# Key/query projection in two 64-column halves, routing behind the first value, an earlier DCT tile and one load queue, in a transformer layer on one core

## The chip, the core and the metric

The kernel runs on one core of one Trainium2 chip. Times are device microseconds (us) of a whole execution. A kernel is timed by several executions; I quote medians with the range. Shares, waits and starts come from one profiled execution of each kernel. Every execution compared here was fast: none was over 1.5% above the fastest of its kernel.

In the profile PE is the matmul engine (PEld is its weight load, which runs beside it: in the kernel before, PE is busy for 98% of the span and PEld for 57%), DVE the vector engine, ACT the scalar engine, POOL GpSimd, and SP the engine that issues most of the transfers. "L181" is line 181 of that kernel's source. Lines shift between kernels, so the text says what each line is.

## The reference

64 audio clips of 80,000 samples become 157 frames of 512 samples each. Cut to what matters:

```python
h = einsum('bfh,kh->bfk', frames, dct_512)          # DCT of each frame
x = layernorm(h)
key   = exp(1j * pi * tanh(x @ Wk + bk))            # 4 sets x 8 planes = 32 columns
query = exp(1j * pi * tanh(x @ Wq + bq))            # 32 columns
V = x @ Wv + bv
for s in range(4):                                  # causal sums of key * V, read by conj(query)
    total += softmax(set_weights)[s] * Re(sum_planes(cumsum(key_s * V) * conj(query_s)))
gate  = sigmoid(x @ Wg + bg)
total = gate * total + (1 - gate) * pos_contrib     # same sums with fixed position phases
h = h + x + (total / norm) @ Wo + bo
x2 = layernorm(h)
scores = softmax(mean_over_frames(x2) @ Wg_ffn + bg_ffn)
e = argmax(scores)                                  # one expert of 16 for each clip
h = h + scores[e] * (x2 @ We[e] + be[e])
```

## The kernel before

All is in 4-byte floats. The 64 clips run in 16 groups of four. A group has five tiles of 128 tokens: the first 128 frames of each clip, and the 29 last ones of all four clips together (the "tails"). DVE and POOL first fold each frame (additions and subtractions of its parts), and PE then does the DCT of the folded frame. Groups are woven together: while the attention of group g runs, the DCT and the first norm of g+1 are made ahead of it, and the experts of g-1 behind it. The causal sums are computed as masked score matrices of phases: scores, times V.

The projection makes 128 columns: key and query, each twice, so that one activation turns one copy into cosines and the other into sines.

```python
def project(g):
    s = S[g]
    s["u"] = u = p1.tile([P, GB, LP], F32, tag="tT", name="u")[:, :, :L]
    ps = psum()
    turns = turn_x2(g - 1)            # transposes of the second norm's tiles
    for k in range(2):                # k: two clips at a time, 314 columns
        next(turns, None)
        next(turns, None)
        for c in range(C):
            nc.tensor.matmul(ps[:, k, : 2 * L], wkq[:, c, :],
                             s["xT"][:, c, 2 * k : 2 * k + 2, :L], ...)
    for _ in turns:
        pass
    nc.scalar.activation(u..., by_halves(ps), AF.Tanh, bias=bkq)

def phasors(g):
    u = S[g].pop("u")
    nc.vector.scalar_tensor_tensor(u, u, sgn, u, ALU.mult, ALU.max)
    rows = slice(2 * F, P)
    nc.scalar.activation(qf[: 2 * F, :, :L], u[rows], AF.Sin, bias=off[rows], scale=scl[rows])
    rows = slice(0, 2 * F)
    nc.scalar.activation(kf[rows, :, :L], u[rows], AF.Sin, bias=off[rows], scale=scl[rows])
    nc.scalar.activation(by_tail(kf_t[rows]), u[rows, :, P:], AF.Sin, ...)
```

Here PE's results go to the memory PSUM, and ACT and DVE empty it (in the profile before, ACT takes 0.79 us for a gate part's 128x628 and DVE 0.32 us for a score's 128x157). Two pools of it matter: `psum()` gives one of three large buffers (two banks each), `bank()` one of two small ones. Transposes, scores and the routing use the small ones.

```python
def scores(i):
    ps = bank()
    nc.tensor.matmul(ps[:, :L], kf[:, i, :P], qf[:, i, :L], start=True, stop=True)
    nc.vector.tensor_tensor(att[i][:, 0, :], ps[:, :L], hmask, ALU.mult)
    ...
# the group's loop, cut to what the change touches
    project(g)
    if behind:
        route(g - 1)                  # 16 matmuls, four 32-column parts of the array at once: 32 records in 1.27 us
    phasors(g)
    if behind:
        route_sum(g - 1)              # DVE
        ...                           # folds of the next frames
        weigh()                       # DVE scales the queries
        for m in range(NM):
            value(g, m)
            if m == 0:
                route_spread(g - 1)
            ...
    for m in range(NM):
        if ahead:
            embed(g + 1, m)           # DCT tile
            if m > 0:
                turn(g + 1, m - 1)    # its transposes; ACT copies the bank away
            embed_ln(g + 1, m)        # statistics, norm, and the addition of bo on POOL
            load_frame(g + 2, m)
        if m < GB:
            gate_part(g, m)
        if m < 2:
            scores(2 * m)
            scores(2 * m + 1)
        ...
```

## Time and profile before

| | before |
|---|---|
| median of 4 executions | 1605.51 us (1604.59 to 1606.74) |
| profiled span, granted PE clock | 1603.6 us, 0.997 |
| distance of two groups (mean from group 2 to 15) | 97.98 us |
| start of the first projection | 46.59 us |
| first projection of group 0 to that of group 1, then to group 2 | 61.19, 99.70 us |

The last rows are read from the starts of the projection's first matmul in each group. As PE is almost never idle, these distances are what the kernel costs, and they can be compared between kernels to some 0.02 us. 14 equal groups make a small term visible that the whole time, with its spread of 2 us, hides. One stretch of the chain of waits is shown here (start, duration, what), where the reads of the attention (L437) meet those of the tails (L450):

```profile
259.21 1.07 PE mm L437 x4
...
260.90 0.50 DVE tT L426
...
261.54 1.02 PE mm L450 x4
262.56 0.44 PE tr L160 x4
```

PE had to wait here until DVE had emptied a large buffer: 3.35 us pass from 259.21 to 262.56. (The chain counts four of the eight L437; the other four run while DVE works, and PE then stands idle for 0.21 us by the timeline.)

### The profile page before, as it was taken

To read this page: it belongs to the slowest core of one execution; us is meant where nothing else is said; L and a number is where in the kernel's file an instruction comes from. 1 tells how busy PE (TensorE), PEld (TensorE's weight loads), DVE (VectorE), ACT (ScalarE), POOL (GpSimd) and SP (SyncE) were. 2 spreads that over 40 slices of the span, in tenths; PEclk is the share of its full clock that TensorE was granted. 3 is DMA by queue.
4 is the path that set the end of the run, shared out by engine and by line. 5 is a ranking of instruction groups with operands and counts; after the bars stand their busy time and mean duration, and the time that the engine had idled before them with its cause. 6 is when DMAs were issued, how large, how long until landed. Compare 5 with 4: busy or idle time off the path is not lost.

```text
span 1603.6 us, 17469 instructions
## 1 busy us (share of the span) xinstructions
PE 1565.5 (98%) x6224; PEld 920.9 (57%) x6224; DVE 713.1 (44%) x1738; ACT 425.2 (27%) x598; POOL 528.8 (33%) x947
## 2 busy tenths in 40 slices
PE   7999999999999999999999999999999999999997
PEld 4656556464564746647465574655646466474652
DVE  4354544435444444444345444354443544444253
ACT  3433123231322313223132232212323132231210
POOL 4424324243332333323234242332424333233032
PEclk9999999999999999999999999999999999999999
DMA  5103131131312313132231411313114131212216
GB/s 181 29 5 132 46 138 46 46 138 55 129 40 77 107 62 129 33 122 62 65 126 40 150 39 54 131 53 131 46 46 138 57 127 40 79 72 62 109 33 203
DMA packets 42998, 135.39 MB, mean 84 GB/s; under 512 B 8016, under 2 KB 8416, under 8 KB 34336
## 3 DMA queue, kind: packets, MB, share of 16 engines
q0 software_dynamic: 15616, 88.09, 16.1%
q1 hardware_dynamic: 26088, 45.66, 9.2%
q8 instruction: 50, 0.82, 0.2%
q10 hardware_dynamic: 1208, 0.52, 0.2%
q14 instruction: 36, 0.29, 0.0%
HBM read 113.67 MB, written 20.58 MB: 84 GB/s over the span
## 4 chain that ended last, share of the span: by engine, by line
PE 89%; DMA 1%; DVE 1%; ACT 1%; issue 1%; POOL 0%; DVEq 0%; POOLq 0%
PE mm L179 45%; PE mm L400 16%; PE mm L437 7%; PE tr L160 4%; PE mm L369 4%; PE mm L196 4%; PE mm L584 3%; PE mm L194 2%; PE mm L450 2%; PE tr L489 1%; PE tr L412 1%; DMA out<-be 1%; ACT x2T L168 1%; DMA be<-in_be,expi 1%; DVE tT L426 0%
## 5 line engine op out<-in xcount | busy, mean ns | idle before, releaser
L400 PE MATMUL mm<-xT,wg 128*128 128x314 f32 x1024 | 281.2, 426 | 0.0
L179 PE MATMUL mm<-wv,xT 128*128 128x512 f32 x512 | 228.4, 598 | 0.9 <-ACT xT L166 0.9
L400 PEld LDWEIGHTS mm<-xT,wg 128*128 128x128 f32 x1024 | 189.1, 188 | 69.7 <-issue 0.5
L179 PE MATMUL mm<-we,x2T 128*128 128x512 f32 x512 | 223.0, 593 | 0.1
L179 PE MATMUL mm<-wo,tT 128*128 128x512 f32 x512 | 222.3, 592 | 0.0
L179 PEld LDWEIGHTS mm<-we,x2T 128*128 128x128 f32 x512 | 97.0, 190 | 122.5 <-issue 118.6
L469 ACT ACTIVATE x<-res,shift,rstd 128x512 f32<-128x512 f32 x80 | 65.1, 813 | 383.7 <-POOL shift L154 383.7
L179 PEld LDWEIGHTS mm<-wo,tT 128*128 128x128 f32 x512 | 97.3, 190 | 117.2 <-issue 114.8
L179 PEld LDWEIGHTS mm<-wv,xT 128*128 128x128 f32 x512 | 95.1, 191 | 112.5 <-issue 110.4
L93 POOL TENSOR_TENSOR frame<-frame 128x256 f32<-128x256 f32 x80 | 58.5, 739 | 292.6 <-DVE even L92 281.7
L151 POOL TENSOR_SCALAR rstd<-mv 128x1 f32<-128x1 f32 x160 | 42.1, 263 | 330.8 <-DVE mv L149 327.9
L437 PE MATMUL mm<-att,v 128*128 128x314 f32 x512 | 143.2, 427 | 0.0
L209 POOL TENSOR_TENSOR res<-res,bo 128x512 f32<-128x512 f32 x80 | 101.7, 1272 | 113.3 <-ACT res L208 110.0
L206 ACT ACTIVATE x<-mm,shift,rstd 128x512 f32<-128x512 f32 x80 | 62.2, 777 | 270.9 <-POOL shift L154 270.7
L466 DVE TENSOR_TENSOR res<-mm,res 128x512 f32<-128x512 f32 x80 | 55.3, 692 | 150.6 <-PE mm L179 150.6
L437 PEld LDWEIGHTS mm<-att,v 128*128 128x128 f32 x512 | 94.9, 190 | 31.2
L592 DVE SCALAR_TENSOR_TENSOR be<-mm,gate,be 128x512 f32<-128x512 f32 x80 | 59.9, 750 | 116.9 <-PE mm L179 76.4
L562 POOL DMA_INDIRECT be<-in_be,expi x80 | 83.3, 1041 | 63.8 <-DMA out<-be 33.0
L147 DVE BATCH_NORM_STATS2 st<-mm 128x6 f32<-128x512 f32 x80 | 55.9, 699 | 106.7 <-PE mm L196 106.7
L152 POOL TENSOR_TENSOR rstd<-rstd,power 128x1 f32<-128x1 f32 x160 | 96.3, 602 | 13.3
L160 PE MATMUL tr<-ident,x 128*128 128x128 f32 x640 | 92.0, 274 | 5.7 <-ACT x L206 3.1
L160 PEld LDWEIGHTS tr<-ident,x 128*128 128x128 f32 x640 | 76.1, 141 | 35.0 <-issue 14.7
(117 smaller groups left out, 1794.3 us busy)
## 6 DMA issues: line engine op xcount, KB each, us to landing
frame<-in_frames SPq DMA_DIRECT2D x80, 256.0 KB
out<-be SPq DMA_DIRECT2D x64, 256.0 KB
out<-be SPq DMA_DIRECT2D x60, 32.0 KB
out<-be SPq DMA_DIRECT2D x60, 26.0 KB
be<-in_be,expi POOLq DMA_INDIRECT x80, 4.1
wv<-in_wv SPq DMA_DIRECT2D x1, 1024.0 KB
wg<-in_wg SPq DMA_DIRECT2D x1, 1024.0 KB
wo<-in_wo SPq DMA_DIRECT2D x1, 1024.0 KB
```

The source lines that it names most:

```text
L152: nc.gpsimd.tensor_tensor(rstd, rstd, power, ALU.pow)
L160: nc.tensor.transpose(tr[:, c * P : (c + 1) * P], x[:, c * P : (c + 1) * P], ident)
L179: nc.tensor.matmul(ps, lhs(c), w[:, c, :], start=(c == 0), stop=(c == C - 1))
L196: nc.tensor.matmul(by_r[:, 1::2, :], ft[:, i, :], dct_o[:, i, :], start=(i == 0), stop=(i == 1))
L206: nc.scalar.activation(x, h, AF.Identity, bias=shift, scale=rstd)
L209: nc.gpsimd.tensor_tensor(r, r, bo, ALU.add)
L369: nc.tensor.matmul(ps[:, k, : 2 * L], wkq[:, c, :], s["xT"][:, c, 2 * k : 2 * k + 2, :L], start=(c == 0), stop=(c == C - 1),)
L400: nc.tensor.matmul(ps[:, k, : 2 * L], wg[:, c, o * P : (o + 1) * P], s["xT"][:, c, 2 * k : 2 * k + 2, :L], start=(c == 0), stop=(c == C - 1),)
L437: nc.tensor.matmul(ps[:, c, : 2 * L], s["v", i][:, cols], att[i], start=True, stop=True)
L469: nc.scalar.activation(x, r, AF.Identity, bias=shift, scale=rstd)
L562: nc.gpsimd.indirect_dma_start(out=be, out_offset=None, in_=a["be"], in_offset=bass.IndirectOffsetOnAxis(ap=s["expi"][:, m : m + 1], axis=0),)
L592: nc.vector.scalar_tensor_tensor(o, ps, s["gate"][:, m : m + 1], o, ALU.mult, ALU.add)
```

## The change

It has four intents. The projection computes only 64 columns, key and query once, and the two pairs of clips are meant to use the two column halves of the array at the same time. The cosines and sines then come from eight smaller activations in place of three. The routing moves behind the first value matmul, which needs nothing new, so that PE doesn't wait for the last copy of x2. The DCT of tile m+1 goes ahead of gate part m, and the transposes of tile m behind it. Last, all loads use one queue, the additions of `bo` in group 0 move off POOL's early work, and there are more warm-up matmuls. Along with this the folds and the scaling of the queries (`weigh`) have other places among the values.

```diff
     def project(g):
-        ps = psum()
+        ps = psum()[:, 0, :]
         turns = turn_x2(g - 1)
-        for k in range(2):
-            next(turns, None)
-            next(turns, None)
-            for c in range(C):
+        for c in range(C):
+            if c % 2 == 0:
+                next(turns, None)
+                next(turns, None)
+            for k in range(2):
                 nc.tensor.matmul(
-                    ps[:, k, : 2 * L],
+                    ps[2 * F * k : 2 * F * (k + 1), : 2 * L],
 ...
     def phasors(g):
-        nc.vector.scalar_tensor_tensor(u, u, sgn, u, ALU.mult, ALU.max)
-        ... (three sines)
+        nc.vector.scalar_tensor_tensor(u[:, 1], u[:, 0], -1.0, u[:, 0], ALU.mult, ALU.max)
+        for n, to in ((0, kf), (1, qf)):
+            for k in range(2):
+                ... (a sine of u[rows, 0] and one of u[rows, 1], 32 rows each)
+        nc.gpsimd.tensor_copy(by_tail(kf_t[: 2 * F]), kf[: 2 * F, :, P:L])
 ...
         project(g)
-        if behind:
-            route(g - 1)
         phasors(g)
-            route_sum(g - 1)
             for m in range(NM):
                 value(g, m)
                 if m == 0:
+                    route(g - 1)
+                    fold_twice(g + 1, 1)
+                    keep_value(g, m)
+                    route_sum(g - 1)
+                elif m == 1:
                     route_spread(g - 1)
 ...
         for m in range(NM):
+            for n in (0, 1) if m == 0 else (m + 1,):
+                if ahead and n < NM:
+                    embed(g + 1, n)
+                    embed_ln(g + 1, n)
+                    load_frame(g + 2, n)
             if ahead:
-                embed(g + 1, m)
-                if m > 0:
-                    turn(g + 1, m - 1)
-                embed_ln(g + 1, m)
-                load_frame(g + 2, m)
+                add_bo(g + 1, m)
             if m < GB:
                 gate_part(g, m)
+                if ahead:
+                    turn(g + 1, m)
             if m < 2:
                 scores(2 * m)
                 scores(2 * m + 1)
 ... (load queue, warm-up, add_bo and the order of the start-up cut)
```

More of the change, by code (lines that the diff above doesn't have):

```diff
@@ L64, in audio_tower, with load @@
     ps_tr = pool("ps_tr", 2, space=bass.MemoryType.PSUM)
-    def load(name, shape, src=None, queue=nc.sync):
+    def load(name, shape, src=None):
         t = const.tile(shape, F32, name=name, tag=name)
-        queue.dma_start(out=t, in_=a[name] if src is None else src)
+        nc.sync.dma_start(out=t, in_=a[name] if src is None else src)
         return t
@@ L111, in audio_tower @@
     load_frame(0, 4)
-    bv = load("bv", [P, D], a["bv"].partition_broadcast(P), queue=nc.scalar)
-    freqs = load("freqs", [2 * PLANES, 1], queue=nc.scalar)
-    ptrig = load("ptrig", [2 * PLANES, 3], queue=nc.scalar)
-    pos = load("pos", [2 * PLANES, LP], queue=nc.scalar)
-    posw = load("posw", [P, 1], a["posw"].partition_broadcast(P), queue=nc.scalar)
-    setw = load("setw", [2 * F, SETS], a["setw"].partition_broadcast(2 * F), queue=nc.scalar)
-    setsel = load("setsel", [2 * F, SETS], queue=nc.scalar)
-    trig = load("trig", [P, 3], queue=nc.scalar)
-    sgn, scl, off = trig[:, 0:1], trig[:, 1:2], trig[:, 2:3]
-    bkq = load("bkq", [P, 1], queue=nc.scalar)
-    hbg = load("hbg", [P, C], a["bg"], queue=nc.scalar)
+    bv = load("bv", [P, D], a["bv"].partition_broadcast(P))
+    freqs = load("freqs", [2 * PLANES, 1])
+    ptrig = load("ptrig", [2 * PLANES, 3])
+    pos = load("pos", [2 * PLANES, LP])
+    posw = load("posw", [P, 1], a["posw"].partition_broadcast(P))
+    setw = load("setw", [2 * F, SETS], a["setw"].partition_broadcast(2 * F))
+    setsel = load("setsel", [2 * F, SETS])
+    hbg = load("hbg", [P, C], a["bg"])
     bo = load("bo", [P, D], a["bo"].partition_broadcast(P))
-    wkq = load("wkq", [P, C, P])
+    wkq = load("wkq", [P, C, 2 * F])
+    bkq = load("bkq", [P, 1])
     hmask = load("hmask", [P, L])
@@ L137, in audio_tower, with warm @@
     nc.gpsimd.memset(power, -0.5)
-    warm = bank()
-    for _ in range(6):
-        nc.tensor.matmul(warm[:, :P], ident, ident, start=True, stop=True)
+    quarter = const.tile([P, 1], F32, name="quarter", tag="quarter")
+    nc.gpsimd.memset(quarter, PI / 2)
+    def warm(n):
+        ps = bank()
+        for _ in range(n):
+            nc.tensor.matmul(ps[:, :P], ident, ident, start=True, stop=True)
     def statistics(h):
@@ L196, in embed @@
             nc.tensor.matmul(by_r[:, 1::2, :], ft[:, i, :], dct_o[:, i, :], start=(i == 0), stop=(i == 1))
-        s["h"] = h
+        s["h", m] = h
     def embed_ln(g, m):
         s = S[g]
-        h = s.pop("h")
+        h = s.pop(("h", m))
         rstd, shift = statistics(h)
@@ L208, in embed_ln, with add_bo @@
         nc.scalar.activation(r, h, AF.Identity, bias=shift, scale=rstd1)
-        nc.gpsimd.tensor_tensor(r, r, bo, ALU.add)
         s["res"].append(r)
         s["x", m] = x
+    def add_bo(g, m):
+        r = S[g]["res"][m]
+        nc.gpsimd.tensor_tensor(r, r, bo, ALU.add)
     def turn(g, m):
@@ L302, in audio_tower @@
     consts = constants()
+    warm(9)
     fold_once(0, 0)
     fold_twice(0, 0)
+    embed(0, 0)
     fold_once(0, 1)
-    embed(0, 0)
     fold_twice(0, 1)
+    embed(0, 1)
     embed_ln(0, 0)
+    warm(6)
     fold_once(0, 2)
-    embed(0, 1)
     embed_ln(0, 1)
@@ L315, in audio_tower @@
     fold_once(0, 3)
+    value(0, 0)
     embed_ln(0, 2)
     fold_twice(0, 3)
-    value(0, 0)
     turn(0, 1)
@@ L352, in audio_tower @@
     keep_value(0, 4)
+    for m in range(NM):
+        add_bo(0, m)
     def by_halves(ps):
@@ L361, in project @@
         s = S[g]
-        s["u"] = u = p1.tile([P, GB, LP], F32, tag="tT", name="u")[:, :, :L]
-        ps = psum()
+        ps = psum()[:, 0, :]
         turns = turn_x2(g - 1)
-        for k in range(2):
-            next(turns, None)
-            next(turns, None)
-            for c in range(C):
+        for c in range(C):
[3 more added lines that the diff above has]
+            for k in range(2):
                 nc.tensor.matmul(
-                    ps[:, k, : 2 * L],
+                    ps[2 * F * k : 2 * F * (k + 1), : 2 * L],
                     wkq[:, c, :],
@@ L375, in project @@
                 )
+        s["u"] = u = p1.tile([P, 2, 2, L], F32, tag="tT", name="u")
+        nc.scalar.activation(u[:, 0], ps[:, : 2 * L].rearrange("p (b t) -> p b t", b=2), AF.Tanh, bias=bkq)
         for _ in turns:
             pass
-        nc.scalar.activation(u.rearrange("p (k b) t -> p k b t", k=2), by_halves(ps), AF.Tanh, bias=bkq)
     def phasors(g):
         u = S[g].pop("u")
-        nc.vector.scalar_tensor_tensor(u, u, sgn, u, ALU.mult, ALU.max)
-        rows = slice(2 * F, P)
-        nc.scalar.activation(qf[: 2 * F, :, :L], u[rows], AF.Sin, bias=off[rows], scale=scl[rows])
-        rows = slice(0, 2 * F)
-        nc.scalar.activation(kf[rows, :, :L], u[rows], AF.Sin, bias=off[rows], scale=scl[rows])
-        nc.scalar.activation(by_tail(kf_t[rows]), u[rows, :, P:], AF.Sin, bias=off[rows], scale=scl[rows])
+        nc.vector.scalar_tensor_tensor(u[:, 1], u[:, 0], -1.0, u[:, 0], ALU.mult, ALU.max)
+        for n, to in ((0, kf), (1, qf)):
+            for k in range(2):
+                rows = slice(2 * F * k + F * n, 2 * F * k + F * (n + 1))
+                nc.scalar.activation(to[F : 2 * F, 2 * k : 2 * k + 2, :L], u[rows, 0], AF.Sin, scale=PI)
+                nc.scalar.activation(
+                    to[:F, 2 * k : 2 * k + 2, :L], u[rows, 1], AF.Sin, bias=quarter[rows], scale=-PI
+                )
+        nc.gpsimd.tensor_copy(by_tail(kf_t[: 2 * F]), kf[: 2 * F, :, P:L])
     def weigh():
@@ L613, in audio_tower @@
             fold_twice(g + 1, 0)
-            weigh()
             for m in range(NM):
@@ L617, in audio_tower @@
                 if m == 0:
+                    route(g - 1)
[3 more added lines that the diff above has]
+                elif m == 1:
                     route_spread(g - 1)
-                keep_value(g, m)
-                if m == 0:
+                    fold_once(g + 1, 2)
+                    keep_value(g, m)
                     pick(g - 1)
                     fetch(g - 1, range(GB))
-                if m == 1:
-                    pick_gate(g - 1)
-                if m + 1 < NM:
-                    fold_twice(g + 1, m + 1)
-                if m + 2 < NM:
-                    fold_once(g + 1, m + 2)
+                    fold_twice(g + 1, 2)
+                else:
+                    if m == 2:
+                        weigh()
+                        pick_gate(g - 1)
+                    if m + 1 < NM:
+                        fold_once(g + 1, m + 1)
+                    keep_value(g, m)
+                    if m + 1 < NM:
+                        fold_twice(g + 1, m + 1)
         else:
             fold_twice(1, 3)
+            fold_once(1, 4)
             weigh()
-            fold_once(1, 4)
             fold_twice(1, 4)
         for m in range(NM):
-            if ahead:
-                embed(g + 1, m)
-                if m > 0:
-                    turn(g + 1, m - 1)
-                embed_ln(g + 1, m)
-                load_frame(g + 2, m)
+            for n in (0, 1) if m == 0 else (m + 1,):
[3 more added lines that the diff above has]
+                    load_frame(g + 2, n)
+            if ahead:
+                add_bo(g + 1, m)
             if m < GB:
                 gate_part(g, m)
+                if ahead:
+                    turn(g + 1, m)
             if m < 2:
@@ L731, in _constants @@
         "dct_o": f(np.stack([odd[:, ahead].T, odd[:, back].T], axis=1)),
-        "trig": trig(F, 2, PI),
         "ptrig": trig(PLANES, 1, 2 * PI),
@@ L764 @@
         "frames": _frames(w["x"]),
-        "wkq": _rows(np.concatenate([wk, wk, wq, wq], axis=1)),
-        "bkq": np.concatenate([bk, bk, bq, bq])[:, None],
+        "wkq": _rows(np.concatenate([wk, wq], axis=1)),
+        "bkq": np.concatenate([bk, bq, bk, bq])[:, None],
         "setw": w["attn_set_weights"],
```

## The prediction

> **What bounds the kernel now.** I read the page first, then the groups of PE by shape, the chain of work in order of time, the waits of PE, and the timeline of one group (199 to 306 us) and of the first 66 us.
>
> ```profile
> PE 1565.5 (98%) x6224; PEld 920.9 (57%) x6224; DVE 713.1 (44%) x1738; ACT 425.2 (27%) x598; POOL 528.8 (33%) x947
> ...
> PE 89%; DMA 1%; DVE 1%; ACT 1%; issue 1%; POOL 0%; DVEq 0%; POOLq 0%
> ```
>
> PE is busy 98% of the span and carries 89% of the chain, with a granted clock of 0.997. So only two things move the time: PE work removed, and gaps on PE opened or closed. The chain gives the real pitch of matmuls (a single record is longer, since matmuls overlap):
>
> ```profile
> 172.14 30.90 PE mm L179 x72
> 203.04 3.57 PE mm L584 x32
> 207.64 2.12 PE mm L369 x8
> 210.62 2.12 PE mm L369 x8
> 213.85 1.27 PE tr L489 x32
> ```
>
> L179 is the full-width matmul of 512 columns: 30.90/72 = 0.429 us per record. L369 is the key/query projection: 2.12/8 = 0.264 us per record, 16 records and 4.23 us per group, all on the path. L584 (expert tails) already uses four 32-column parts of the array: 32 records in 3.57 us is 8 steps of 0.429 plus 0.14. So parts do run at once, at full pitch. L369 recurs every 97.98 us: one group of batches. From the shapes I count 96.6 us of matmul streaming in it, so it holds 1.4 us of gaps. The waits name them:
>
> ```profile
> PE tr L489 <- ACT x2T L168: 10.8, 16, 0.7
> PE mm L194 <- DVE frame L100: 6.7, 2, 4.2
> PE tr L160 <- ACT x L206: 3.1, 3, 1.7
> PE mm L450 <- DVE tT L426: 3.1, 15, 0.2
> ```
>
> The first and last recur in each group; the others are start-up. From start to start, the routing gap is 0.84 us (the transposes of the last x2 tile stop streaming at 213.01, L489 starts at 213.85) and the L450 gap 0.37 us.
>
> [...] Read instruction by instruction, the last full matmul before L584 starts at 202.45 and the first narrow one at 202.97, 0.09 more than a pitch; leaving costs 0.11, plus 0.03 and 0.05 of slower first instructions: 0.29 us per excursion. [...] here the four starts lie 7 ns apart, also negligible. [...] here the clock over 10 to 20 us is 0.84, and 0.81 over 20 to 30, around the 4.24 us gap at 13.6. [...]
>
> **The change, part by part.**
>
> *Projection in halves.* 16 records in 8 steps: 8 x 0.264 = 2.12 us saved. The transposes of x2 cut it in two sections, so two excursions at 0.29 come back: net 1.54 us per group; 1.8 in group 0, which has no transposes there.
>
> *Routing behind value 0.* Value 0 needs nothing new, so the 0.84 us gap closes; entering the narrow mode, hidden by the gap before, now costs 0.12. Net 0.72 us. The tail's own routing is unchanged.
>
> *Phasors.* Eight sines of 32 x 314 replace three. 64x628 takes 0.91, 64x116 takes 0.47, so 0.86 ns per column: 0.64 each, some 0.54 apart, 4.3 us instead of 2.2. ACT is 27% busy: off the path, except in group 0. But the copy of the key tails goes to POOL ahead of the folds, the folds precede value 0's eviction and the routing sum on DVE, and the routing spread on PE needs that sum. Going through these with the durations of 213 to 219 us I get the sum 12.7 us after the first transpose and PE at the spread after 12.9. About even; I charge 0.1 us.
>
> *DCT ahead, and the transposes.* Before: DCT tile m, transposes of tile m-1, gate part m, scores. After: DCT tile m+1, gate part m, transposes of tile m, then scores. Three tiles in a row (transposes, score, score) now need the two small PSUM banks. The order in which ACT serves them is fixed: gate tanh, then the copy that frees the transposes' bank.
>
> ```profile
> 233.86 4.39 PE L400 MATMUL mm<-xT,wg 128*128 128x314 f32 x16
> 238.09 0.69 PE L412 MATMUL tr<-qf,kf 128*128 128x157 f32 x4
> 238.29 0.79 ACT L408 ACTIVATE gT<-mm,hbg 128x628 f32<-128x628 f32 x1 [0.49 <-PE mm L400]
> 238.56 0.32 DVE L413 TENSOR_TENSOR att<-tr,hmask 128x157 f32<-128x157 f32 x1 [3.58 <-PE tr L412]
> ```
>
> Count from the end of the gate part, E (here 238.09). Transposes take 0.44, the first score 0.27, so PE wants a third bank at E+0.70. The tanh starts at E+0.20, the copy 0.69 later (61.30 and 61.99 in group 0), takes 0.58 and ends at E+1.47; PE resumes 0.05 later, with 0.1 of weight load exposed: E+1.62, a wait of 0.92. If the allocator gives the bank of the first score instead, DVE reads that from E+0.91 to 1.23 and PE resumes near 1.45: 0.75. I take 0.84, twice per group (tiles 0 and 1): 1.68 us. Before, the scores followed the gate directly and found both banks free. On the other side the L450 gap should go: DCT tile 4 is evicted a whole gate part earlier, so a large bank is free: 0.37.
>
> *Start-up.* `bo` (needed early, landed late) stalls POOL, and PE behind it:
>
> ```profile
> 15.47 1.26 POOL L209 TENSOR_TENSOR res<-res,bo 128x512 f32<-128x512 f32 x1 [3.27 <-DMA bo<-in_bo]
> ...
> 17.80 1.22 PE L194 MATMUL mm<-dct_e,frame 128*128 128x128 f32 x4 [4.24 <-DVE frame L100]
> ...
> 21.09 4.99 PE L179 MATMUL mm<-wv,xT 128*128 128x512 f32 x8 [0.37 <-ACT xT L166]
> ```
>
> With that addition taken out, the third DCT tile can start near 12.5 instead of 17.8, and the first value near 15.5 instead of 21.1; at full clock that value takes 3.4 instead of 4.8. The extra warm-up matmuls fill waiting time. The single load queue puts 8 short issues of some 0.45 us ahead of `bo` and the weights, which PE needs only after 35 us. I estimate the first projection 7.5 us earlier (9 if all goes well).
>
> *Group 0.* Without routing there is no value work over the phasors. DVE waits for the last of eight sines (6.4 us after the projection) before it scales the queries, and only then takes the statistics of the first DCT tile; its x is ready near 10.6. PE has two DCT tiles and a gate part, 6.8 us, then waits some 3.8 us for the transposes, with perhaps 1.5 us of lower clock after it, and 1.6 at the banks. Before, the wait here was 1.2. Worse by 5.7.
>
> *Sum.* Groups 1 to 14: 1.54 + 0.72 + 0.37 - 1.68 - 0.10 = 0.85 us each, 11.9. Group 15 has no DCT ahead: 2.3. Group 0: 1.8 - 5.7. Start-up: 7.5. Together 11.9 + 2.3 - 3.9 + 7.5 = 17.8 us: 1606.2 - 17.8 = 1588.4, say 1588.
>
> **The rivals.**
> 1. *No bank wait* (a score finds a bank, or I have the order of ACT wrong). Then 1.68 x 14 + 1.6 = 25 us more are gained: 1563, faster by 2.7%. For it: the tuner moved the transposes there on purpose. Against: two banks, three tiles in a row, and no reader that can finish within 0.7 us.
> 2. *The halves do not overlap*: nothing saved, excursions paid: 2.12 x 16 = 34 us worse, 1622. Against: L584 and L489 overlap four parts at full pitch, and weights of 32 columns (0.11 us) load beside the matmuls; 64 columns should too, with 0.264 us to hide in.
> 3. *A later wait takes more*: the routing sum reaches PE late by 0.5 us and not 0.1, or the third score waits for a copy behind ACT's sines, table load and group-0 evictions (3 us more). Some 9 us: 1597.
> 4. *Start-up held by loads*: 95% DMA share between 10 and 20 us leaves little room; the gain there could be 2 us: 1594.
>
> **Range and chances.** Rival 1 or a milder form of it sets the low end, rivals 3 and 4 together the high end: 1565 to 1603. The 2% line is 1574.1; it is passed only if the bank wait is mostly absent or the start-up gains far more than I think: 0.20. Slower by 2% (over 1638) needs rival 2 and more: 0.02. Within 2%: 0.78.
>
> **What would show it.** Right: the projection takes about 1.06 us of chain in each of two sections; the routing wait on ACT is gone; PE waits at the scores' line for ACT (or DVE) some 28 to 30 times, 0.6 to 0.9 each (less in the profile's own count, which starts at the record's end); L450's wait is gone; the period is near 97.1 us; group 0 shows a PE wait of 3 to 4 us at the transposes. Wrong: a period of 95.5 (no bank wait) or above 98 (no overlap, or a bigger wait), or a wait at the routing spread of more than 0.3 us per group.

## The result, and the profile after

The changed kernel takes 1580.63 us (median of 4, 1579.34 to 1580.90) against 1605.51. The ratio is 0.9843, with a 95% interval of 0.9826 to 0.986. A ratio here is the mean time of one kernel's fast runs over that of the other's of the same rounds, so it isn't quite the ratio of the medians. The kernel is faster by 1.6%, which is in the class "within 2%"; the predicted time of 1588.0 was 7.4 us too long, and the range held it.

The page of the changed kernel answers to the two lines shown of before:

```profile
PE 1544.8 (98%) x6242; PEld 891.7 (57%) x6242; DVE 706.0 (45%) x1738; ACT 446.2 (28%) x678; POOL 529.5 (34%) x964
...
PE 96%; DVE 1%; DMA 1%; ACT 1%; POOL 1%; issue 0%; SPq 0%; DVEq 0%; POOLq 0%
```

PE is busy 98% as before, in a shorter span: its busy time is 20.7 us less and the span 26.0, so most of the gain is work taken off PE and not idle time filled. ACT has the extra sines (678 instructions against 598) and doesn't mind, as a whole: it is busy 28% of the span against 27%. The chain of waits shows where in a group the time went. This is the stretch from the experts' tails (L598) of one group to the reads of the attention (L451) and of the tails (L464):

```profile
197.18 3.57 PE mm L598 x32
200.75 1.02 PE tr L162 x8
201.77 1.21 PE mm L379 x8
202.98 1.02 PE tr L162 x8
204.00 1.21 PE mm L379 x8
205.21 0.59 PE tr L162 x4
205.80 3.44 PE mm L181 x8
209.23 1.21 PE tr L503 x32
...
227.21 4.23 PE mm L414 x16
231.44 0.44 PE tr L162 x4
231.87 0.28 PE tr L426 x2
...
232.56 0.54 PE tr L426 x2
233.09 0.44 PE mm L196 x4
...
252.46 2.12 PE mm L451 x8
254.57 0.78 PE mm L464 x4
255.36 0.44 PE tr L162 x4
```

Each section of the projection (L379) takes 1.21 us where it took 2.12. The value (L181) follows the last transposes at once, and the routing (L503) comes behind it with no wait. The reads of the attention meet those of the tails without a gap: 2.90 us from 252.46 to 255.36 against 3.35, so 0.45 us less. One thing is new: the two scores of a pair (L426) are no longer one piece. The waits of PE say what lies between them (what waited, on what: us in total, times, longest):

```profile
PE tr L426 <- DVE att L427: 12.5, 30, 0.5
PE tr L162 <- ACT x L208: 3.4, 2, 3.0
PE tr L162 <- ACT x2T L168: 3.2, 3, 2.4
...
PE tr L503 <- ACT x2T L170: 0.7, 1, 0.7
```

The first is the bank wait that the prediction put in: 30 times, but on DVE, which reads the first score's bank, and not on ACT. The timeline shows it (start, duration, engine, line, operation, and in brackets the idle time ahead with what ended it):

```profile
231.28 0.60 PE L162 MATMUL tr<-ident,x 128*128 128x128 f32 x4
...
231.71 0.43 PE L426 MATMUL tr<-qf,kf 128*128 128x157 f32 x2
...
232.18 0.32 DVE L427 TENSOR_TENSOR att<-tr,hmask 128x157 f32<-128x157 f32 x1 [4.02 <-PE tr L426]
232.56 0.54 PE L426 MATMUL tr<-qf,kf 128*128 128x157 f32 x2 [0.42 <-DVE att L427]
```

The transposes took one small bank and the first score the other; the second score starts 0.06 us after DVE has read the first. The routing's old wait is down to one, that of the last group. The second and third lines of the waits are single ones: 3.0 us in group 0 and 2.4 us in group 1.

The time is accounted for by these distances:

| | before | after | gained |
|---|---|---|---|
| start of the first projection | 46.59 | 37.52 | 9.07 |
| from there to group 1 | 61.19 | 63.48 | -2.29 |
| from group 1 to group 2 | 99.70 | 100.70 | -1.00 |
| 13 distances, groups 2 to 15 | 13 x 97.98 | 13 x 96.64 | 17.4 |
| from group 15's projection to the end | 122.41 | 119.53 | 2.88 |

The sum, 26.0 us, is the difference of the profiled spans (1603.6 less 1577.6).

The granted clock moved some of this too. At the start it was 0.84 (10 to 20 us) and 0.81 (20 to 30 us) before, and it is 1.00 in both now. In groups 0 and 1 it is the other way round: behind the waits of 3.0 and 2.4 us the changed kernel had 0.83 over 50 to 60 us and over 100 to 110 us, where the kernel before had 1.00 throughout both groups. At 0.83 some 1.7 us of 10 are lost, if PE has work throughout (an estimate). So the distances of groups 0 and 1 hold to some 2 us only: e5, whose edit acts from group 1 on, has 65.07 us in place of 63.48 from group 0 to group 1, with 0.66 over 50 to 60 us.

### The profile page after: what moved, and what is told of

It is laid out like the page before. It is cut to its first block, busy times and chain, and to the rows that moved or that the text cites. A ratio compares the mean times of both kernels' runs of the same rounds, so it can differ in the third digit from the quotient of the medians.

```text
span 1577.6 us, 17597 instructions
## 1 busy us (share of the span) xinstructions
PE 1544.8 (98%) x6242; PEld 891.7 (57%) x6242; DVE 706.0 (45%) x1738; ACT 446.2 (28%) x678; POOL 529.5 (34%) x964
## 4 chain that ended last, share of the span: by engine, by line
PE 96%; DVE 1%; DMA 1%; ACT 1%; POOL 1%; issue 0%; SPq 0%; DVEq 0%; POOLq 0%
PE mm L181 49%; PE mm L414 17%; PE mm L451 9%; PE tr L162 5%; PE mm L198 4%; PE mm L598 3%; PE mm L379 2%; PE mm L196 2%; PE tr L426 2%; PE mm L464 2%; PE tr L503 1%; DVE att L427 1%; DMA out<-be 0%; DMA be<-in_be,expi 0%; DMA frame<-in_frames 0%
## 5 line engine op out<-in xcount | busy, mean ns | idle before, releaser
L414 PEld LDWEIGHTS mm<-xT,wg 128*128 128x128 f32 x1024 | 192.6, 188 | 71.8 <-issue 0.5
L181 PE MATMUL mm<-wv,xT 128*128 128x512 f32 x512 | 229.5, 596 | 1.5 <-ACT xT L168 1.5
L181 PE MATMUL mm<-we,x2T 128*128 128x512 f32 x512 | 222.9, 593 | 0.0
L181 PE MATMUL mm<-wo,tT 128*128 128x512 f32 x512 | 222.3, 592 | 0.0
L181 PEld LDWEIGHTS mm<-we,x2T 128*128 128x128 f32 x512 | 97.0, 190 | 122.3 <-issue 118.6
L181 PEld LDWEIGHTS mm<-wo,tT 128*128 128x128 f32 x512 | 97.3, 190 | 117.2 <-issue 114.8
L181 PEld LDWEIGHTS mm<-wv,xT 128*128 128x128 f32 x512 | 93.5, 190 | 104.6 <-issue 102.7
L451 PE MATMUL mm<-att,v 128*128 128x314 f32 x512 | 143.2, 427 | 0.0
L451 PEld LDWEIGHTS mm<-att,v 128*128 128x128 f32 x512 | 94.9, 190 | 31.2
L439 DVE TENSOR_TENSOR tT<-mm,gT 128x314 f32<-128x314 f32 x128 | 62.3, 487 | 90.3 <-PE mm L451 84.8
L401 POOL COPY kf_t<-kf 64x116 f32<-64x116 f32 x16 | 4.4, 278 | 269.3 <-ACT kf L398 269.3
```

What stands on the lines that cost most here:

```text
L181: nc.tensor.matmul(ps, lhs(c), w[:, c, :], start=(c == 0), stop=(c == C - 1))
L414: nc.tensor.matmul(ps[:, k, : 2 * L], wg[:, c, o * P : (o + 1) * P], s["xT"][:, c, 2 * k : 2 * k + 2, :L], start=(c == 0), stop=(c == C - 1),)
L439: nc.vector.tensor_tensor(to, reads[0], th, ALU.mult)
L451: nc.tensor.matmul(ps[:, c, : 2 * L], s["v", i][:, cols], att[i], start=True, stop=True)
```

## The experiments

The theory was the prediction's own sum: a projection worth 1.5 us and a routing wait worth 0.7 per group, a new wait for small banks that takes much of it back, a start-up that `bo` had held, and eight sines that cost group 0. The rivals put each of these elsewhere. Diffs are against the changed kernel. All times are medians of 4 or 5 executions; the kernel before ran beside them each time at 1605.0 to 1605.4 us.

### e1_turn_later: the transposes moved off the scores

```diff
+            if ahead and m > 0:
+                turn(g + 1, m - 1)
             if ahead:
                 add_bo(g + 1, m)
             if m < GB:
                 gate_part(g, m)
-                if ahead:
-                    turn(g + 1, m)
```

> One edit to the changed kernel (1580.6 us): the transposes of tile m stand behind the next DCT tile and ahead of gate part m+1, no longer between gate part m and the scores. Theory (the two small PSUM banks: transposes and two scores in a row want three): the wait of PE at the scores, 0.68 us from start to start in two places of 15 groups (20 us), goes, and nothing takes its place: 1560 us, period 95.3 us. In group 0 the wait for x stays, at the DCT tile or the transposes. Rival (the order is there for a reason: without it PE waits for x or for a large bank in every group): the wait moves to the transposes or the DCT tiles and the time stays at 1575 to 1582.

Measured: 1558.88 us, ratio to before 0.971 (0.9694 to 0.9726), distance of groups 95.28 us. The wait at the scores' line is gone from the list. Against the changed kernel the distance is 1.37 us shorter: two waits per group, 0.68 each.

### e2_one_bank: the pair of scores in one bank, transposes left where they are

```diff
     def scores(i):
         ps = bank()
-        nc.tensor.matmul(ps[:, :L], kf[:, i, :P], qf[:, i, :L], start=True, stop=True)
+        for n in range(2):
+            nc.tensor.matmul(ps[:, n * LP : n * LP + L], kf[:, i + n, :P], qf[:, i + n, :L], ...)
+        for n in range(2):
             ... (evictions of i + n)
             if m < 2:
                 scores(2 * m)
-                scores(2 * m + 1)
```

> One edit to the changed kernel (1580.6 us): the order stays, but the two scores of a pair are written side by side into one small bank, so that transposes and scores want two banks and not three. Theory (number of banks): the wait at the scores goes, 1560 us, period 95.3. Rival (PE waits at the second score for something else that the score reads, or the evictions on DVE are late): the wait stays, 1579 to 1582. If DVE now starts its first eviction 0.13 us later, that costs nothing on PE.

Measured: 1559.17 us, ratio 0.9713 (0.9697 to 0.973), distance 95.28 us, the same as e1 to the last digit. In the chain the pair is one piece again, and the DCT follows:

```profile
228.17 0.44 PE tr L162 x4
228.61 0.54 PE tr L427 x4
229.14 0.44 PE mm L196 x4
```

From the transposes to the DCT it is 0.97 us (228.17 to 229.14) where the changed kernel needs 1.65 (231.44 to 233.09): 0.68 again. Two different edits, one of which moves nothing in the order of PE's tiles, give the same distance. So the cost is the third small tile in a row with two banks, and not where the transposes stand. It also shows how a wait is to be counted: the list of waits has 12.5 us for 30 of them, 0.42 each, but each costs 0.68, since the list counts from the end of a record and leaves out the slower first records behind the gap (the score's two take 0.54 us there against 0.43). The distances decide.

### e3_projection_undone: projection and sines as before, all else as changed

```diff
-    for c in range(C): ... for k in range(2): ps[2 * F * k : 2 * F * (k + 1), : 2 * L]
+    for k in range(2): ... for c in range(C): ps[:, k, : 2 * L]
-        ... (eight sines and the copy on POOL)
+        ... (three sines)
```

> Projection and phasors as in the kernel before, all else as changed (1580.6 us). Theory (the halves save 1.35 us in each of 15 groups and 1.95 in group 0, start to start of the traces): 1603 us, period 98.0. Rival A (the shorter projection only fills time that PE would have waited anyway, as at the bank or the routing sum): less than 10 us slower. Rival B (the eight sines cost elsewhere, as in group 0, where DVE waits for the last of them): some 3 us of the 22 come back, 1600.

Measured: 1597.71 us, ratio 0.9956 (0.9939 to 0.9973), distance 98.16 us. So the halves are worth 98.16 - 96.64 = 1.52 us per group. The chain has the same stretch as above:

```profile
198.10 1.02 PE tr L164 x8
199.12 2.12 PE mm L380 x8
201.24 0.87 PE tr L164 x8
202.11 2.12 PE mm L380 x8
204.23 0.44 PE tr L164 x4
204.66 3.44 PE mm L183 x8
```

The transposes behind a full-width projection take 0.87 and 0.44; behind the halves they take 1.02 and 0.59. Leaving the narrow mode (matmuls of 64 columns) cost 0.15 us each time here. A section of halves takes 1.21 where four steps of 0.264 would be 1.06: entering cost 0.15 too. So an excursion (into the narrow mode and back) cost 0.30, and 2 x (2.12 - 1.21 - 0.15) = 1.52.

In the whole time, though, undoing the halves costs only 17.1 us, while 1.52 for each of 15 groups and 1.95 for group 0 (its projection takes 4.22 us in the kernel before and 2.27 in the changed one) would be 24.8. The first two groups explain most of that. The distance from group 0 to 1 is 61.11 here and 63.48 in the changed kernel. Without its own projection group 0 takes 56.89 here and 61.21 there, so the eight sines cost group 0 4.3 us, the lower clock behind the wait included (1.00 here over 50 to 60 us). From group 1 to group 2 it is 99.88 here, 1.72 over this kernel's own usual distance, as it is in the kernel before (99.70 against 97.98). In the changed kernel it is 100.70, which is 4.06 over, 2.3 more. So in this execution group 1 got nothing from the shorter projection. The traces show two reasons. PE waits for a copy of x2 between the two sections, 1.4 us here and 2.4 in the changed kernel: group 1 has no experts between the last norms and these transposes, and a shorter section covers less of the wait. And behind it the changed kernel was granted a clock of 0.83 over 100 to 110 us. e1 and e2 below have the same wait of 2.4 us with a clock of 1.00 over these 10 us, and their group 1 is 2.48 us over the usual distance. So of the 2.3 us some 0.8 are the longer wait and 1.6 the clock. No run changes either by itself. 24.8 less 4.3 and 2.3 is 18.2; about 1 us stays unlocated, less than the spread of this kernel's four executions (1596.83 to 1599.15).

### e4_halves_in_sequence: the two halves one after the other in the queue

```diff
-        for c in range(C):
-            if c % 2 == 0:
-                next(turns, None)
-                next(turns, None)
-            for k in range(2):
+        for c0 in range(0, C, 2):
+            next(turns, None)
+            next(turns, None)
+            for k, c in ((0, c0), (0, c0 + 1), (1, c0), (1, c0 + 1)):
```

> The changed kernel (1580.6 us) with the matmuls of each section in another order: both slices of one half, then both of the other, so that neighbours in the queue use the same 64 columns. Theory (a matmul starts only after those ahead of it in the queue, so halves overlap only where neighbours differ): 7 steps of 0.264 us in a section and not 4, 1.6 us more per group, 25 us: 1606. Rival (PE takes the matmuls of the free half ahead from its queue): no difference, 1580 to 1582.

Measured: 1581.21 us, ratio 0.9851 (0.9835 to 0.9868), distance 96.65 us: the same as the changed kernel, as the rival had it. The built program has PE's matmuls in the diff's order, and the starts of records that run together lie 13 ns apart in place of 7. A matmul here is two records (8 matmuls in the code, 16 records per group in the trace). If each had to wait until the one ahead of it in the queue had started, a section would be at least six steps in place of four, 2 x 0.264 = 0.53 us more by my estimate (seven, as I had expected, if this holds record by record). The chain of this kernel shows none of it:

```profile
202.73 1.22 PE mm L378 x8
203.95 1.02 PE tr L162 x8
```

So in this run the matmuls of the free half did not wait for the earlier ones of the busy half: 1.22 us for this section, 1.21 with alternating order. (The trace doesn't name the half of a record; this is read from the length of the section.)

### e9_same_half: all in one half but the last matmul

```diff
-        ps = psum()[:, 0, :]
+        both = psum()
+        ps = both[:, 0, :]
+                last = k == 1 and c == C - 1
-                    ps[2 * F * k : 2 * F * (k + 1), : 2 * L],
+                    ps[2 * F :, : 2 * L] if last else both[: 2 * F, k, : 2 * L],
 ... (start and stop set to match)
```

> A control with a wrong result on purpose: as the changed kernel (1580.6 us), but both slices go through the same 64 columns of the array (one matmul excepted, that fills the other half once). Theory (what runs at once are the two halves of the array, whatever the order in the queue): nothing overlaps, a section takes about 2.1 us and not 1.06, some 1.9 us more per group, 1609 us. Rival (with 64 columns two records of one float32 matmul overlap by themselves, in one half too, which would explain why the order made no difference): 1580 to 1583.

Measured: 1603.62 us, ratio 0.9988 (0.9973 to 1.0003), distance 98.21 us, 1.57 more than the changed kernel. The result is wrong, as meant (relative error 0.133). The same 64-column matmuls now take, from their start to that of the next transposes, 2.26 us in the first section and 1.73 in the second:

```profile
202.62 2.33 PE L381 MATMUL mm<-xT,wkq 128*64 128x314 f32 x8
204.88 1.09 PE L162 MATMUL tr<-ident,x 128*128 128x128 f32 x8
205.90 1.80 PE L381 MATMUL mm<-xT,wkq 128*64 128x314 f32 x8
207.63 0.55 PE L162 MATMUL tr<-ident,x 128*128 128x128 f32 x3
```

That is eight steps and six, each with the excursion's 0.15. My expectation of 1.9 forgot the one excepted matmul, which runs beside another: six steps more than the changed kernel, 6 x 0.264 = 1.58, is what was measured. So the gain here comes from the two halves working at once. The narrower weights alone gave nothing: 98.21 us per group, against 98.16 in e3 at full width.

### e5_route_undone: routing back ahead of the values

```diff
         project(g)
+        if behind:
+            route(g - 1)
         phasors(g)
         if behind:
+            route_sum(g - 1)
 ...
                 if m == 0:
-                    route(g - 1)
-                    route_sum(g - 1)
```

> The changed kernel (1580.6 us) with routing and its sum back ahead of the first value, as in the kernel before. Theory (the routing waits for the copy of the last x2 tile; moving it behind value 0 saves 0.77 us start to start in 15 groups, what is left of 2.28 after the 1.51 that undoing the projection showed): 1592 us, PE waiting 0.6 to 0.7 for ACT ahead of the routing in every group. Rival (with the shorter projection the copy is no longer late, or value work only moves the wait to the routing spread): within 3 us of 1580.6.

Measured: 1591.88 us, ratio 0.9914 (0.9898 to 0.9931), distance 97.38 us. The move is worth 0.74 us per group. The old wait is back in the list of PE's waits, with the numbers of the kernel before:

```profile
PE tr L503 <- ACT x2T L170: 10.8, 16, 0.7
```

### e6_bo_early: the addition of bo in group 0 back at its old place

```diff
         nc.scalar.activation(r, h, AF.Identity, bias=shift, scale=rstd1)
+        if g == 0:
+            nc.gpsimd.tensor_tensor(r, r, bo, ALU.add)
 ...
-    for m in range(NM):
-        add_bo(0, m)
```

> The changed kernel (1580.6 us) with the addition of bo in group 0 back where it was, right behind each residual on GpSimd. Theory (this in-order wait for the load of bo is what held the start): GpSimd waits for bo at the first tile, the third DCT tile is held, and the first projection, at 37.5 us now, starts 4 to 6 us later: 1585 to 1587. Rival (the start was gained by warm-up matmuls and the load order): first projection within 1.5 us of 37.5, time within 2 us.

Measured: 1589.36 us, ratio 0.9905 (0.9888 to 0.9921). The first projection starts at 47.44 us, 9.9 later than in the changed kernel and 0.85 later than before the change. PE waits at a DCT for a frame that POOL, held at the addition, has not folded:

```profile
PE mm L196 <- DVE frame L100: 6.8, 2, 6.5
```

```profile
16.25 1.26 POOL L212 TENSOR_TENSOR res<-res,bo 128x512 f32<-128x512 f32 x1 [5.52 <-DMA hmask_t<-in_hmask_t]
```

POOL stood idle for 5.52 us until a load had landed. The profile names `hmask_t`, which is issued behind `bo` on the same queue; that `bo` was what it waited for is read from the code. Undoing this one move takes back the whole gain of the start-up. The 0.85 us beyond it say nothing of the rest of the new start-up: they are within the spread of such starts (see e7), and the clock differed as well (0.72 and 0.77 over 10 to 20 and 20 to 30 us, against 0.84 and 0.81). In the time the move is worth 8.7 us.

### e7_two_queues: the small loads back on a second queue

```diff
-    def load(name, shape, src=None):
+    def load(name, shape, src=None, queue=nc.sync):
-    bv = load("bv", [P, D], a["bv"].partition_broadcast(P))
+    bv = load("bv", [P, D], a["bv"].partition_broadcast(P), queue=nc.scalar)
     ... (likewise freqs, ptrig, pos, posw, setw, setsel, hbg, bkq)
```

> The changed kernel (1580.6 us) with the nine small loads and bv back on the ACT queue. Theory ([...] bv on the second queue delays the first frame from 3.6 to 5.1 us): the first DCT tile and with it the first projection come 1 to 1.6 us later, 1582. Rival (a second queue helps, since 8 issues of 0.45 us no longer stand ahead of the weights): the projection starts as early or earlier than 37.5 and the time is 1579 to 1580.6.

Measured: 1580.08 us, ratio 0.9842 (0.9825 to 0.9858): the same. The first frame came earlier with one queue. The bracket of the first fold gives its landing, 5.27 us here:

```profile
5.27 0.43 DVE L92 TENSOR_TENSOR even<-frame 128x256 f32<-128x256 f32 x1 [5.27 <-DMA frame<-in_frames]
```

In the changed kernel the same fold starts at 3.56 us. Of these 1.7 us nothing clear is left at the first projection: 38.42 against 37.52, where the other variants with the new start-up (e1 to e5 and e8 to e11) lie from 37.82 to 38.45. In the time there is no difference.

### e8_weigh_late: in group 0 the queries scaled just ahead of the scores

```diff
             fold_once(1, 4)
-            weigh()
             fold_twice(1, 4)
 ...
+            if m == 0 and not behind:
+                weigh()
             if m < 2:
                 scores(2 * m)
```

> The changed kernel (1580.6 us); in group 0 alone the scaling of the queries, which waits for the last of the eight sines, stands behind the statistics of the first two DCT tiles on DVE. Theory (eight sines hold DVE in group 0 and through it PE: a wait of 3.0 us at the transposes, then 10 us at a clock of 0.83): the wait falls below 1 us, the clock stays at 1.00, 1575 us. Rival (ACT itself is late: x stands behind the sines there too): 1579 to 1581. The undone projection came back 7 us short of its 24.6, which this should explain.

Measured: 1577.88 us, ratio 0.9834 (0.9818 to 0.9851). Group 0 takes 60.91 us in place of 63.48, so 2.6 us come back, and 2.75 in the time: half of what I expected. The timeline of the changed kernel shows the wait that this is about:

```profile
45.97 0.54 DVE L404 TENSOR_SCALAR qf<-qf,wvec 64x628 f32<-64x628 f32 x1 [2.70 <-ACT qf L398]
...
49.09 0.78 ACT L208 ACTIVATE x<-mm,shift,rstd 128x512 f32<-128x512 f32 x1 [3.16 <-POOL shift L156]
...
49.92 0.66 PE L162 MATMUL tr<-ident,x 128*128 128x128 f32 x4 [3.02 <-ACT x L208]
```

DVE waits 2.70 us for the last sine before it scales the queries, the statistics stand behind that, then POOL's small steps, then the norm on ACT, and PE waits 3.02 us. With the scaling moved the wait is 1.8. The clock of that stretch shows the rest (us, busy time of PE, PEld, DVE, ACT and POOL with counts, granted clock, DMA share, GB/s), first the changed kernel, then e8:

```profile
50.00:60.00 10.00, 9.08 (x39) 7.01 (x40) 3.08 (x8) 7.19 (x10) 4.28 (x9) 0.83 0.09 28
```

```profile
50.00:60.00 10.00, 9.08 (x46) 7.16 (x46) 4.29 (x11) 6.51 (x9) 3.64 (x6) 1.00 0.08 28
```

PE is equally busy in both, but after the 3.0 us wait it gets through 39 records at a clock of 0.83, and after the shorter one through 46 at 1.00. The lower clock didn't follow such a wait every time: e6 has the same wait of 3.02 us in group 0 and 1.00 over the 10 us from 60, and its group 0 takes 62.14 us. So of the 2.6 us some 1.2 (62.14 less 60.91) are the shorter wait, and the rest goes with the clock. The remaining wait of 1.8 us shows that the scaling was not all. It doesn't come from ACT, which in e8 stands idle for 1.94 us ahead of the norm, until POOL's small steps give the shift. These steps need the statistics from DVE, and ahead of the statistics DVE waits 1.59 us for a fold on POOL, which stands behind the copy of the key tails and so behind the fourth sine. No run took that away.

### e10_narrow_together: all three narrow steps side by side, with e1 and e8

```diff
 (e1 and e8, and:)
-        turns = turn_x2(g - 1)
+        turns = S[g - 1].pop("turns", None) or turn_x2(g - 1)   # most are now done between the experts
+        early = g > 1
+        if early:
+            route(g - 1)              # right behind the experts' tails, ahead of the projection
         project(g)
 ...
             for m in range(NM):
                 expert(g - 1, m)
+                for _ in range((0, 2, 2, 1, 0)[m]):
+                    next(turns)       # the transposes of x2
```

> For a version that beats both: transposes ahead of the gate part one tile later (as in the run that took the bank wait away, 1558.9), late scaling in group 0, and from group 2 on all transposes of x2 stand between the experts, so that expert tails, routing and projection follow each other in narrow mode: one excursion in place of four. Theory (each excursion [...] costs 0.3 us): 0.8 us less per group in 14 groups, 11 us, and some 5 from group 0: 1543. Rival ([...] ACT's copies between the experts delay something): 1552 to 1556.

Measured: 1553.98 us (1551.33 to 1554.18), ratio 0.9675 (0.9661 to 0.9688), distance 95.07 us, only 0.21 less than e1. Experts' tails, routing and projection now follow each other without full-width work between them, but a new wait took most of it:

```profile
PE tr L516 <- DVE tot L510: 3.4, 13, 0.3
```

The routing spread (L516) waits for the routing sum on DVE, which still stood behind the folds and the first value's eviction.

### e11_sum_first: the same, with the routing sum right behind the projection

```diff
 (e10, and:)
         project(g)
+        if early:
+            route_sum(g - 1)
 ...
-                    route_sum(g - 1)
+                    if not early:
+                        route_sum(g - 1)
```

> The version with the narrow modes together (1554.0 us, period 95.07) and one edit: from group 2 on the routing sum is taken on DVE right behind the projection, not behind the folds and the eviction of value 0. There PE waited for it at the routing spread in 13 groups, 0.26 us each by the records and some 0.4 from start to start. Theory (this wait ate most of the 0.8 us that one excursion in place of four should save): period 94.5, 1546 us. Rival ([...] little was saved): period 95.0, 1553.

Measured: 1545.28 us (1544.69 to 1545.99), ratio 0.9625 (0.9612 to 0.9638), distance 94.54 us, correct. The wait is gone:

```profile
193.17 3.64 PE L598 MATMUL mm<-we,x2T 128*32 128x512 f32 x32
196.63 1.25 PE L503 MATMUL tr<-x2T,rwg 128*32 128x157 f32 x32
197.81 2.33 PE L379 MATMUL mm<-xT,wkq 128*64 128x314 f32 x16
200.07 7.13 PE L181 MATMUL mm<-wv,xT 128*128 128x512 f32 x16
```

The four narrow pieces of a group (tails, two sections, routing) have become one run of three. Against e1 it saves 0.74 us per group. On the chain the projection's 16 records still take 2.26 us, 0.15 over eight steps of 0.264, so going over from 32 to 64 columns is paid like entering from full width. This version beats both kernels: 3.75% under the kernel before by the ratio, and 2.2% under the changed one by the medians.

## Why the prediction was right or wrong

The prediction was right in its class and range, and the ledger of a usual group closes. Each measured term has its own experiment, except the last two:

| per group, us | predicted | measured | from |
|---|---|---|---|
| projection in halves, net of two excursions | 1.54 | 1.52 | e3 |
| routing behind the first value | 0.72 | 0.74 | e5 |
| wait for small banks, both tiles | -1.68 | -1.37 | e1, e2 |
| gap between the two kinds of reads | 0.37 | 0.45 | the two chains |
| routing spread late | -0.10 | 0 | no such wait in the list |
| sum | 0.85 | 1.34 | 97.98 - 96.64 |

**The halves.** Rival 2 (no overlap) is out: e9 shows what it would look like (2.26 us for its first section), and in e4 not even the order in the queue made a difference (96.65 us per group against 96.64). The excursion, estimated at 0.29 from the experts' tails (its four terms add up to 0.28), measures 0.30.

**The term that was mis-sized is the bank wait.** The mechanism was right: three small tiles, two banks, no reader done in time. The step that failed is "I take 0.84, twice per group": it is the mean of two cases, ACT's copy of the transposes (0.92) and DVE's read of the first score (0.75), because I did not know which bank the allocator would give. It gave the score's bank, and the runs show 0.68 even for that: I had 0.22 us from the end of DVE's read to the next score, and the trace has 0.06 to its start and 0.11 of slower records (0.54 against 0.43). Over the 13 distances from group 2 on the step makes 13 x 0.31 = 4.0 of the 7.4 us by which I was off. The two smaller terms of the table, 0.08 and 0.10, make 2.3 more, and the start-up 1.6.

**Rival 1**, no bank wait, was put at 1563 us. e1 and e2 are that kernel: 1558.9 and 1559.2. So the bank wait alone kept the change from being faster by over 2%, and it came from moving the transposes, the one part of the change with no gain of its own in a usual group. (The gap between the reads closes by the DCT's move, which e1 keeps.)

**Start-up.** I had 7.5 us, "9 if all goes well", and it was 9.07 (8.1 to 8.8 by the starts of the variants with the same start-up). e6 confirms the reason, the addition of `bo` on POOL. The third DCT tile starts at 11.62 us, where I had 12.5. Of the clock I counted 1.4 us, at the first value alone; 0.84 and 0.81 over 10 us each are up to 3.5 us of lost clock (an estimate), and all of it went. Rival 4, start-up held by loads, is out, and the single queue did nothing either way in the time (e7).

**Group 0.** "1.8 - 5.7" was a net loss of 3.9; measured 2.29. The chain of causes held (sines, scaling, statistics, norm, PE's wait, lower clock), with a wait of 3.0 us where I had 3.8. e3 measures the sines' cost at 4.3, where my terms without the banks make 4.1 (3.8 - 1.2 + 1.5, of which the 1.5 for a lower clock was my estimate), and e8 gets 2.6 of it back. But the clock didn't drop behind such a wait every time: in e6 it was 1.00 behind 3.02 us.

**Group 1** is where the prediction had a hole: I treated it like the others (+0.85), and it lost 1.00: I had not counted the wait for x2 between the sections, nor the lower clock behind it. That the errors in groups 0 and 1 nearly cancel, -3.05 predicted and -3.29 measured, is luck.

**Rival 3** (a later wait takes more) did not come in the changed kernel, but it did in e10, with exactly the wait that the prediction named, at the routing spread.

## What to carry to other kernels

When an engine is busy all the time, first look whether the granted clock was the same, and then compare the distance between two equal stages of two traces and not the whole times: terms of 0.1 us become visible, and each part of a change can be undone and priced by itself. Count the small PSUM tiles that follow each other without other work between them: one more than there are banks cost a wait for a reader here, 0.68 us in each of 30 places, and putting two small results into one bank was enough to avoid it (e2: 95.28 us per group against 96.64). Gather narrow matmuls of several purposes into one stretch, because each way into and out of the narrow mode was paid for here (0.15 us), and then look again at who feeds the step behind them.
